# Two-layer text-and-image attention: five value products instead of six for two entries, image tokens first in every other entry, small work moved between VectorE and GpSimd, and a new order of the first groups

## The chip, the cores and the metric

The kernel runs on one core of one Trainium2 chip, in one launch. The metric is the device time of the execution in microseconds; the figure of a kernel is the median of its runs. The engines are TensorE (PE; PEld is its weight load), VectorE (DVE), ScalarE (ACT), GpSimd (POOL) and SyncE (SP, which only issues DMAs here).

## The reference

Two layers of cross attention run one after the other on `x`, 16 entries of 256 tokens by 320 channels, with 20 heads of 16. Each entry has a context of 256 tokens by 512; in layer 0 its first 77 tokens are text and the other 179 are image tokens, in layer 1 the last 4 are image tokens. This is layer 0, shortened:

```python
text, ip = ctx[:, :77], ctx[:, 77:]
q = x @ Wq; k_text = text @ Wk; v_text = text @ Wv
text_out = softmax(q_h @ k_h.T * scale) @ v_h                 # by head
ip_k = ip @ Wk_ip; ip_v = ip @ Wv_ip
text_probs = softmax(q @ k_text.T * scale)                    # all channels
sem = (text_probs @ text) @ ip.T * scale                      # query x image token
ip_out = (softmax(q_h @ ip_k_h.T * scale + 0.5 * sem) * mask) @ ip_v_h
out = (text_out + ip_out) @ Wout + bout + x
```

Layer 1 has the same form with a normalized `sem`.

## The kernel before, in words

Numbers are fp32, and most products are made of fp32r halves: a value is rounded to a high part by ACT and the rest is its low part, a subtraction on DVE or POOL (`halves` L162, `split` L280). `prod` (L236) then makes high x high, high x low and low x high; over 512 channels, four blocks of 128, that is 12 matmuls.

**Layer 0 by groups.** A group k is four heads of one entry (5 groups an entry, 80 in layer 0). `slot0` (L785) writes the PE order out by hand: the scores of group k+2 (`score0` L739), whose maxima DVE takes from PSUM for text and image tokens apart; the turned scores of group k (`turned0` L760: token by query), to which the maxima have been added as rows by a DMA (`maxima0` L750); exp on ACT; a factor on POOL (L776) that carries `sem`; and the values of group k-1 (`attend0` L778, three blocks V of tokens times P), which DVE transposes and divides by the sums in `settle0` (L813) before POOL adds text and image into `hsn`. The values have one PSUM bank, P, for all groups, so the next group's values wait until the last reader of the bank is done. The scores have one bank pair, S.

**What is prepared meanwhile.** Two entries (a pair c) share the products of the context. The tasks of a pair are spread over the groups ahead by due times (`task`, L1149 on; `shifted(n, ...)` is in groups relative to the pair's first one, n = 10 c), and `fill` runs what is due: `k0` loads the context (`context` L265, tiles `cta` and `ctb`, split whole in 512 columns: text and image of one entry, then of the other) and makes the keys (`keys0` L367), which go out to DRAM (`kd`) and back as rows of `ks`; `q0` the queries (`queries0` L647, `hq` being x in halves), out to `qd` and back into `qs`; `v0` the values of one entry (`values0_` L419): three products of 128 context rows by 320 columns, rows 0 to 127 with the text weights, the same rows with the image weights, and rows 128 to 255 with the image weights; in the first two a mask per row (`tmask`) drops the tokens of the other kind; `m0t` the token product M (`tokens0` L431); `s0` the factor (`semantic0` L654). `c0` (`finish` L839) splits the finished heads of an entry into `ho` and makes the output product (`project` L604, L611).

**Order.** PE's order is the program's. In `begin` (L1247), which is all that comes before group 0's slot, the order of SP, ACT, DVE and POOL is the program's too; after it a scheduler sets the order of these, but instructions marked `queued` stay behind the last `anchor` of their engine (a maximum on DVE, an exp on ACT, a factor on POOL). SP issues in order, and a DMA whose data isn't ready holds up those behind it. In `begin`, `stacks0` loads the rows of a group in parts: K (keys), Q (queries), T and M (the factor's rows).

**Layer 1** has no products of that kind; its value step (`settle1` L998) ends with a copy of the last block of `hsn` on POOL.

## Time and profile before

| | |
|---|---|
| median of 3 runs (lowest to highest) | 1493.27 us (1488.1 to 1494.71) |
| profiled execution, its span | 1491.16 us, 1489.3 us |
| granted clock of PE over the span | 0.984 |
| instructions | 36118 |
| first turned scores of group 0 | 56.62 us |
| ten groups of layer 0 (group 34 to 44, first turned matmul each) | 74.50 us |
| HBM read, written | 118.04 MB, 77.04 MB |

The span is that of the profiled execution and begins with its first instruction. Times in rows of the profile are microseconds from there. A row of a timeline or of the chain gives start and length, then engine, line and tiles (written <- read) and how many; a row of a group gives busy us and the mean ns of one instruction, and behind the second bar the idle time of the engine ahead of it with what ended it. A matmul's length in a group runs from its issue to its end, and several are under way at once, so what it costs the path is read from the chain.

### The profile page before, as it was taken

The page shows a single profiled execution, that of the slowest core. Times are in us where ns is not written, and L with a number is a line of the kernel's source. Part 1 is how long each engine was busy: PE and PEld are TensorE (multiplying, and loading weights), DVE is VectorE, ACT ScalarE, POOL GpSimd, SP SyncE. Part 2 cuts the span into 40 slices and gives each one's busy share as a digit, 9 for nine tenths or more (in the row PEclk, how much of TensorE's full clock was granted, in tenths as well). Part 3 has the DMA queues.
Part 4 walks back from the last instruction along what each step waited for, and adds up shares of the span by engine and source line. Part 5 has one row for each costly group of instructions (what it writes and reads, how often), then busy time and mean ns, then how long its engine had stood idle before and what let it go on. Part 6 is the DMA issues. An engine that isn't in the chain of part 4 may idle for free.

```text
span 1489.3 us, 36118 instructions
## 1 busy us (share of the span) xinstructions
PE 1426.1 (96%) x12740; PEld 1155.8 (78%) x12740; DVE 1172.7 (79%) x2595; ACT 886.0 (59%) x1975; POOL 1212.5 (81%) x1302
## 2 busy tenths in 40 slices
PE   8799999999999899789999999999999999999998
PEld 7678888888888788577777777777777777777766
DVE  5467777777777787778887788788878887888787
ACT  5346565656565555456665666566666665666563
POOL 4359797979797877798698779878987898788887
PEclk9799999999999999799999999999999999999999
DMA  7867777778787776684534444444444444444411
GB/s 237 212 178 222 205 223 205 222 204 224 200 228 202 208 204 176 165 222 151 155 104 126 123 117 119 133 122 116 121 133 119 121 121 124 125 122 102 112 32 55
DMA packets 230986, 234.32 MB, mean 157 GB/s; under 512 B 39127, under 2 KB 200678, under 8 KB 230790
## 3 DMA queue, kind: packets, MB, share of 16 engines
q1 hardware_dynamic: 228598, 230.71, 55.8%
q8 instruction: 102, 1.67, 0.5%
q10 hardware_dynamic: 2208, 1.30, 0.4%
q14 instruction: 78, 0.64, 0.1%
HBM read 118.04 MB, written 77.04 MB: 131 GB/s over the span
## 4 chain that ended last, share of the span: by engine, by line
PE 75%; DVE 8%; DMA 5%; POOL 5%; issue 3%; ACT 3%; SPq 1%; ACTq 0%; DVEq 0%; POOLq 0%
PE X L944 15%; PE X L241 14%; PE P L805 6%; PE X L611 5%; PE S L746 5%; PE P L956 5%; PE P L966 4%; PE T L770 4%; PE T L895 3%; PE S L901 3%; PE X L614 2%; PE X L251 2%; PE X L580 2%; DVE mn L748 2%; POOL P L776 1%
## 5 line engine op out<-in xcount | busy, mean ns | idle before, releaser
L776 POOL TENSOR_TENSOR P<-P,rs 128x512 f32<-128x512 f32 x320 | 414.4, 1318 | 86.6 <-ACT P L773 79.8
L935 POOL TENSOR_TENSOR wt<-P,ctb 128x512 f32<-128x512 f32 x318 | 408.4, 1308 | 74.1 <-ACT ctb L933 74.0
L944 PE MATMUL X<-ctb,gm 128*128 128x512 f32 x1120 | 306.3, 402 | 5.8 <-DVE wt L945 5.7
L773 ACT ACTIVATE P<-T 128x512 f32<-128x512 f32 x320 | 175.4, 594 | 159.4 <-PE T L770 112.4
L945 DVE TENSOR_TENSOR wt<-X,wt 128x512 f32<-128x512 f32 x320 | 216.1, 681 | 42.2 <-PE X L944 37.3
L944 PEld LDWEIGHTS X<-ctb,gm 128*128 128x128 f32 x1120 | 195.0, 188 | 39.3 <-DVE wt L945 8.7
L915 ACT ACTIVATE P<-T 128x512 f32<-128x512 f32 x320 | 173.1, 593 | 75.1 <-PE T L895 72.1
L933 ACT ACTIVATE ctb<-P 128x512 fp32r<-128x512 f32 x320 | 186.6, 627 | 38.0 <-PE X L944 35.2
L903 DVE TENSOR_REDUCE mn<-S 128x4 fp32r<-128x1008 f32 x160 | 191.5, 1197 | 0.0
L748 DVE TENSOR_REDUCE mn<-S 128x4 fp32r<-128x716 f32 x160 | 142.4, 890 | 0.0
L805 PE MATMUL P<-P,vr 128*32 128x256 f32 x1920 | 125.9, 393 | 6.1 <-DVE tmp L822 2.2
L746 PE MATMUL S<-ks,qs 125*128 125x256 f32 x640 | 117.4, 307 | 6.2 <-DMA ks<-M 4.1
L746 PEld LDWEIGHTS S<-ks,qs 125*128 125x128 f32 x640 | 89.0, 195 | 40.8 <-issue 22.1
L1035 POOL TENSOR_TENSOR r<-u,rs 128x40 f32<-128x40 f32 (+2 forms) x17 | 108.7, 6395 | 3.1 <-DVE u L1032 3.0
L770 PE MATMUL T<-qs,ks 127*128 127x256 f32 x640 | 107.7, 291 | 0.4 <-DMA qs<-mt 0.3
L747 DVE TENSOR_REDUCE mn<-S 128x4 fp32r<-128x308 f32 x160 | 74.5, 466 | 31.1 <-PE S L746 31.0
L816 DVE STREAM_TRANSPOSE nt<-P 128x512 f32<-128x512 f32 x80 | 57.1, 713 | 52.9 <-PE P L805 52.2
L805 PEld LDWEIGHTS P<-P,vr 128*32 128x32 f32 x1920 | 56.7, 112 | 47.4 <-POOL P L776 7.3
L770 PEld LDWEIGHTS T<-qs,ks 127*128 127x128 f32 x640 | 91.6, 197 | 1.7 <-DMA qs<-mt 0.8
L956 PE MATMUL P<-P,v1t 128*32 128x256 f32 x1280 | 85.7, 385 | 0.0
L966 PE MATMUL P<-wt,zone 128*32 128x256 f32 x1280 | 84.4, 379 | 0.0
L241 PE MATMUL X<-wC,cta 128*128 128x324 f32 (+1 forms) x474 | 78.4, 312 | 0.0
(305 smaller groups left out, 2976.8 us busy)
## 6 DMA issues: line engine op xcount, KB each, us to landing
qd<-q SPq DMA_DIRECT2D x96, 256.0 KB
qs<-tph SPq DMA_DIRECT2D x64, 320.0 KB
rawc<-in_cT_dram SPq DMA_DIRECT2D x60, 256.0 KB
qs<-qd SPq DMA_DIRECT2D x80, 192.0 KB
ks<-kd SPq DMA_DIRECT2D x80, 192.0 KB
ks<-kd SPq DMA_DIRECT2D x160, 96.0 KB
qs<-qd SPq DMA_DIRECT2D x160, 96.0 KB
kd<-kst SPq DMA_DIRECT2D x57, 256.0 KB
```

What stands on the lines that cost most here:

```text
L241: last = mm(out, lhs(a, k), rhs(b, k), start=i == 0, stop=i == len(terms) - 1)
L746: mm(sp[:, h], Q[: XROW + T0, h, t * 128 : (t + 1) * 128], K[: XROW + T0, h], start=True, stop=True)
L770: mm(st[p][:, j], K[:KS0, 2 * p + j, t * 128 : (t + 1) * 128], Q[:KS0, 2 * p + j], start=True, stop=True)
L773: exp = anchor(nc.scalar.activation(pt, st[p], AF.Exp, scale=SCALE))
L776: anchor(nc.gpsimd.tensor_mul(pt, pt, rs[:, t : t + 1].to_broadcast([128, 2, S])))
L805: mm(pv[32 * s : 32 * s + 32, o : o + S], v[:, vt, h : h + 32], P[k, s // 2][:, t, s % 2], start=vt < 2, stop=vt != 1,)
L903: anchor(nc.vector.tensor_reduce(maxes[k + 2][:, t], sp[:, :, :T1], axis=AX.X, op=ALU.max))
L915: anchor(nc.scalar.activation(P[k, u][:, t], st[u], AF.Exp, scale=SCALE))
L933: nc.scalar.activation(R[k, u][:, t], P[k, u][:, t], AF.Copy, scale=0.5)
L935: anchor(eng.tensor_sub(W[k, u][:, t], P[k, u][:, t], f(R[k, u][:, t])))
L944: mm(yp, gm[:, gb], R[k, u][:, kt], start=i == 0, stop=i == len(blocks[n]) - 1)
L945: nc.vector.tensor_mul(W[k, u][:, n], yp, W[k, u][:, n])
```

## The change

**Context layout.** `cta` and `ctb` hold, for high and low part each, the text columns of both entries (2 x 77) and the image columns of both (2 x 179) with 26 zeroed columns between the two image parts. The split therefore runs in two pieces, text and image (each with one ACT and one POOL or DVE instruction; `begin` likewise). The text keys take 154 columns, the token product 180 instead of 192.

**Values.** In even entries the image tokens come first: tokens 0 to 127 of the image, then 51 image and 77 text tokens. In odd entries it is 77 text and 51 image tokens, then 128 image tokens. The 51 image rows of both lie in one tile of 128 rows, so one product (`vm`) makes both; each entry keeps a text product and one of 128 image rows. The masks of V are written per entry by POOL (`mark`, two copies), where `marks` wrote them once.

**Order of tokens.** For even entries the key stacks are read at an offset of 77 columns (`turned_ks`), the maxima change sides, and the values take the blocks image, mixed image, text. M's zero columns are set once and no longer by a memset for each entry.

**Keys.** The image parts of `kst` are evacuated in two pieces, the copy of the text keys to `kb` is made by two instructions.

**Between engines.** In `settle0` the product goes to the values' bank and a DVE sum over it writes `hsn` (twice in the last group of an entry, for POOL's copy). The last block of `hq` is subtracted by POOL on 64 partitions, where DVE made one instruction on 128. In layer 0 the low part of `ho` is made by POOL (`split_pool`). In layer 1 the last group writes both copies in one DVE product.

**The start.** The second entry's products stand between the scores of groups 0 and 1; the writes of its queries (`held`) and of its keys come behind the maxima of group 1; the second pair's splits move out of `begin` into group 0.

```diff
     def evacuate(hi, lo, out, m, pieces=None):
+        cut = [lambda t, b=b: t[:, b] for b in pieces] if pieces else [lambda t: t]
...
+        for of in cut:
+            nc.scalar.copy(of(hi), of(out[:64] if m == 2 else out))
...
+        for of in cut:
+            nc.vector.tensor_sub(of(out if m == 2 else lo), of(out), f(of(hi)))
```
```diff
+    def value_rows(ct, at, w, *to):
+        vp = bank()[:, :320]
+        prod(vp, lambda s, k: side(ct[k], s, at, 128), lambda s, k: w(s, k), 4)
+        for V, t, sc in to:
             nc.scalar.activation(
                 vcols(V, V0W)[:, t, :, 0:16], vp.rearrange("p (h d) -> p h d", d=D), AF.Copy, scale=sc
             )
     def values0_(b):
         ct, i = ct0[b // 2], b % 2
-        V = vr[(b + 2) % 3]
-        for t, (w,), lo, sc in ((0, wv0, 0, tmask[:, 0:1]), (1, wvi0, 0, tmask[:, 1:2]), (2, wvi0, 128, 1.0)):
...
+        V = mark(b)
+        value_rows(ct, T0 if i else -MIX, wv0[0], (V, 0, masks(b)[0]))
+        yield
+        value_rows(ct, CI + (CG + MIX if i else 0), wvi0[0], (V, 2, 1.0))
+        yield
         return V
+    def values_mixed(c):
+        to = [(vr[(b + 2) % 3], 1, masks(b)[1]) for b in (2 * c, 2 * c + 1)]
+        value_rows(ct0[c], CI + 128, wvi0[0], *to)
+        yield
```
```diff
-        tmp = buf("tmp", [128, 2, 8, 16], bufs=2)
-        nc.vector.tensor_mul(tmp, nt[:, :, :, 0:16], rz.unsqueeze(3).to_broadcast([128, 2, 8, 16]))
-        nc.gpsimd.tensor_add(hn[:, g // 2, :, g % 2], tmp[:, 0], tmp[:, 1])
+        tmp = pv[:, 16:272]
+        nc.vector.tensor_mul(
+            tmp.rearrange("p (a f d) -> p a f d", a=2, f=8), nt[:, :, :, 0:16], rz.unsqueeze(3).to_broadcast([128, 2, 8, 16])
+        )
+        tmp = tmp.rearrange("p (a f d) -> p f d a", a=2, f=8)
         if g == NG - 1:
-            nc.gpsimd.tensor_copy(hn[:, 2, :, 1], hn[:, 2, :, 0])
+            for i in range(2):
+                nc.vector.tensor_reduce(hn[:, 2, :, i], tmp, axis=AX.X, op=ALU.add)
             later(0.45, lambda: gather(0, b))
+        else:
+            nc.vector.tensor_reduce(hn[:, g // 2, :, g % 2], tmp, axis=AX.X, op=ALU.add)
+    def split_pool(src, neg, tag):
+        hl = buf(tag, [128, 5, S], FR)
+        nc.scalar.copy(hl[:, 0:2], src[:, 0:2])
+        nc.scalar.activation(hl[:, 2], src[:, 2], AF.Copy, scale=neg)
+        nc.gpsimd.tensor_sub(hl[:, 3:5], src[:, 0:2], f(hl[:, 0:2]))
+        nc.gpsimd.tensor_add(hl[:, 2], src[:, 2], f(hl[:, 2]))
+        return hl
```
```diff
-        task(("v0", 2 * c), shifted(n, -7, -5.4, -5), lambda b=2 * c: values0_(b), *k)
-        task(("v0", 2 * c + 1), shifted(n, -4, -3.8, -3.4), lambda b=2 * c + 1: values0_(b), *k)
+        task(("v0", 2 * c), shifted(n, -7, -5.4), lambda b=2 * c: values0_(b), *k)
+        task(("vm", c), shifted(n, -4.2), lambda c=c: values_mixed(c), *k)
+        task(("v0", 2 * c + 1), shifted(n, -3.8, -3.4), lambda b=2 * c + 1: values0_(b), ("vm", c))
```
```diff
         stacks0(1, "TQK")
-        parts(v0)
         get(*v0)
+        parts(vm)
+        stacks0(2, "KQ")
+        parts(q1)
+        score0(0, 0)
+        stacks0(2, "TM")
         parts(v1)
-        stacks0(2, "KQ")
-        score0(0, 0)
-        parts(q1)
-        stacks0(2, "TM")
+        score0(0, 1)
         get(*q1)
         parts(s1, s1, s1)
-        score0(0, 1)
+        stacks0(3, "KQ")
+        maxima0(0, nc.sync)
+        stacks0(3, "TM")
         parts(k1)
         parts(s1, s1)
-        parts(k0)
-        parts(v1)
-        maxima0(0, nc.sync)
-        parts(s1)
+        score0(1, 0)
         parts(v1)
         get(*v1)
-        score0(1, 0)
-        parts(k1)
         parts(s1)
-        stacks0(3)
-        parts(k1)
         score0(1, 1)
-        parts(k1, k1)
+        parts(s1)
         maxima0(1, nc.sync)
+        for make in held:
+            make()
+        parts(k0)
         resid0.append(load(xT_d[0], "xc"))
```

More of the change, by code (lines that the diff above doesn't have):

```diff
@@ L200, in in_turn @@
             if i:
-                halves(*ahead.pop(0), eng, wait)
+                hi, lo, src = ahead.pop(0)
+                if isinstance(hi, list):
+                    for piece in zip(hi, lo, by_side(src)):
+                        halves(*piece, eng, "pieces")
+                else:
+                    halves(hi, lo, src, eng, wait)
             for j in new:
@@ L301, in xattn2 @@
     for k in range(4):
-        first["c", k] = cT_d[k * 128 : (k + 1) * 128, : 2 * S], ct[k][:, 0], ct[k][:, 1], ("rawc", "raw")[k // 2]
+        first["c", k] = cT_d[k * 128 : (k + 1) * 128, : 2 * S], *[[of(ct[k], s) for of in (texts_of, images_of)] for s in range(2)], ("rawc", "raw")[k // 2]
         first["k", k] = rows(wk0_d, k), *rounded(wkt[:, k]), "P"
@@ L396, in keys_first @@
         out = lambda lo, hi: bank()[:, : 2 * (hi - lo)].rearrange("p (b t) -> p b t", b=2)
-        kp = [out(0, T0 + 1) for m in range(3)]
+        kp = [out(0, T0) for m in range(3)]
         for k in range(4):
@@ L616, in project, with queries @@
             yield
-    def queries(l, a):
+    def queries(l, a, held=None):
         qh = buf("q", [128, 2, 3, S], FR)
+        send = lambda out, in_: dma(out, in_) if held is None else held.append(lambda: dma(out, in_))
         def evac(m, pp):
@@ L649, in queries0 @@
         yield
-        xs = split(x, tmask[:, 5:6], nc.gpsimd, "hq") if b else xs0.pop()
+        xs = split(x, None, nc.gpsimd, "hq") if b else xs0.pop()
         yield
-        return (yield from queries(0, xs))
+        return (yield from queries(0, xs, held if b == 1 else None))
     def semantic0(b):
@@ L1264, in high @@
             for n in names:
-                nc.scalar.copy(first[n][1], view(n))
+                for hi, src in zip(first[n][1], by_side(landed[n])) if n[0] == "c" else ((first[n][1], view(n)),):
+                    nc.scalar.copy(hi, src)
         def low(*names, eng=nc.vector):
             for n in names:
+                if n[0] == "c":
+                    for hi, lo, src in zip(first[n][1], first[n][2], by_side(landed[n])):
+                        eng.tensor_sub(lo, src, f(hi))
+                    continue
                 lo = first[n][2]
```

207 lines of the change are left out of this document (132 added, 75 removed).

## The prediction

> **What bounds the kernel now.** I read the busy shares first, then the same engines by stage (windows), then the chain of waits inside one stage, and last the groups of that stage.
>
> ```profile
> PE 1426.1 (96%) x12740; PEld 1155.8 (78%) x12740; DVE 1172.7 (79%) x2595; ACT 886.0 (59%) x1975; POOL 1212.5 (81%) x1302
> ```
> ```profile
> 0.00:60.00 60.00, 46.51 (x273) 43.46 (x274) 32.06 (x94) 30.86 (x80) 19.74 (x43) 0.92 0.84 239
> ```
> ```profile
> 337.23:367.60 30.37, 30.14 (x287) 25.95 (x286) 23.50 (x57) 19.70 (x48) 30.32 (x29) 1.00 0.81 233
> ...
> 322.67:397.17 74.50, 73.44 (x702) 63.60 (x701) 57.95 (x137) 44.31 (x105) 65.72 (x65) 1.00 0.78 214
> 500.00:690.00 190.00, 168.03 (x1506) 137.50 (x1508) 149.19 (x330) 100.92 (x238) 154.65 (x175) 0.93 0.69 190
> 690.00:1489.00 799.00, 783.70 (x6953) 605.47 (x6943) 661.08 (x1403) 499.96 (x1062) 661.92 (x725) 1.00 0.41 116
> ```
> ```profile
> by line: PE X L241 23.6%; PE P L805 17.4%; PE S L746 15.6%; PE T L770 11.3%; PE X L611 8.1%; issue 3.2%; PE X L668 3.1%; PE X L251 2.9%; PE X L614 2.4%; DVE mn L748 2.2%; PE X L754 1.5%; ACT cta L166 1.4%; ACT ho L284 1.0%; DVE ho L285 0.9%
> ```
>
> The windows give, after the length, busy us of PE, PEld, DVE, ACT and POOL, then clock and DMA share. There are four regimes. Up to 60 us the start: PE is idle for 13.5 us. Then layer 0, which repeats every two entries; one period is 74.50 us (322.67 to 397.17), with PE busy 73.44. From 500 to 690 us the weights of layer 1 come in on top, and PE has 22 us of idle time. From 690 us layer 1, PE busy 784 of 799. The by-line row is the chain of the one period: nearly all of it is PE, with X L241, the products of the context, as its largest line. So in layer 0 time taken from PE is time taken from the span, as long as nothing else is as full. One thing is: in the stretch 337.23 to 367.60 (groups 36 to 39 of that period), POOL is busy 30.32 of 30.37 us, beside a full PE. That is where this change is decided.
>
> **The change part by part.**
>
> *One value product fewer for two entries (PE, removed).* Each entry had three products of 12 matmuls over 320 columns; the mixed rows of two entries now share one, so two entries need five instead of six.
>
> ```profile
> 326.47 3.52 PE X L241 x24
> ...
> 387.88 2.86 PE X L241 x24
> ```
> ```profile
> L241 PE MATMUL X<-wD,cta 128*128 128x320 f32 x24 | 4.2, 309 | 0.0
> ```
>
> The first row, from the chain, is two such products in a row: 3.52 / 24 = 0.147 us a matmul on the path (the 309 ns of the group row is its length from issue to end, and neighbours overlap). A product is 12 x 0.147 = 1.76 us. The second row is one product of 320 columns behind one of the token product's 192 columns, so the latter has (2.86 - 1.76) / 12 = 0.091 us each; at 180 columns I estimate 0.086, 0.12 us for two entries. Seven of the eight pairs lie in layer 0's periods (the first is in the start, below): 7 x 1.88 = 13.2 us of PE work less. The Trainium skill, "TensorE: Matmul & The Clock Gate", section Back-to-back issue gap, gives N / 2.4 + 2.5 ns for a lone warm matmul, so 136 ns at 320 columns; the row's 147 ns is longer, and by the page the seven products would be worth 11.4 us instead of 12.3.
>
> *GpSimd (POOL): low parts in, sums out.* Groups of the one period:
>
> ```profile
> L776 POOL TENSOR_TENSOR P<-P,rs 128x512 f32<-128x512 f32 x42 | 54.2, 1315 | 7.8 <-ACT P L773 7.7
> L823 POOL TENSOR_TENSOR hsn<-tmp 128x128 f32<-128x128 f32 x10 | 5.1, 508 | 0.5 <-DVE tmp L822 0.5
> ...
> L285 POOL TENSOR_TENSOR hq<-xq,hq 128x512 fp32r<-128x512 f32 x2 | 2.6, 1290 | 0.0
> L386 POOL CAST kb<-kst 128x308 fp32r<-128x308 f32 x2 | 0.9, 440 | 0.0
> L825 POOL COPY hsn<-hsn 128x128 f32<-128x128 f32 x2 | 0.6, 289 | 0.0
> L436 POOL MEMSET M<- 77x154 f32 x2 | 0.5, 227 | 0.5 <-PE X L698 0.5
> ```
>
> Removed per period: 10 sums of 0.508, 2 copies of 0.289, 2 memsets of 0.227: 6.1 us. Added: two low parts of ho, each 512 elements (1.29, as hq) and 256 elements, which lie between the 128-element and the 512-element row; on their line (2.04 ns an element) 0.77. Together 2 x 2.06 = 4.1. The last block of hq twice: I take 0.77 for it too, bounds 0.51 and 1.29, 1.5. Context splits in two pieces (154 and 358 elements, 0.56 + 0.98 on the line) in place of one of 512: 0.25 x 4 = 1.0. The key casts in halves, 128 elements being 0.289 and 308 being 0.440: 0.18 x 3 = 0.5. Four marks of 20 columns, about a memset each: 0.9. Added 8.0, net +1.9 us per period on 65.7.
>
> *VectorE (DVE).* Groups of the same period:
>
> ```profile
> L747 DVE TENSOR_REDUCE mn<-S 128x4 fp32r<-128x308 f32 x20 | 9.3, 466 | 2.0 <-PE S L746 1.8
> ...
> L285 DVE TENSOR_TENSOR ho<-hT,ho 128x512 fp32r<-128x512 f32 x2 | 2.3, 1165 | 1.4 <-ACT ho L284 1.4
> L286 DVE SCALAR_TENSOR_TENSOR ho<-ho,tmask,hT 128x256 fp32r<-128x256 f32 x2 | 2.2, 1102 | 0.0
> L286 DVE SCALAR_TENSOR_TENSOR hq<-hq,tmask,xq 128x256 fp32r<-128x256 f32 x2 | 1.3, 640 | 0.0
> ```
>
> It loses 5.8 us of ho and hq and gets 12 sums over 256 elements out of PSUM. No row shows that sum; it lies between nothing and the 0.466 of 308 elements, I take 0.41 (nearest is the product of the same size below, 0.41): 4.9 us. With image parts evacuated in two pieces (about +0.4) it comes out even, at 58 of 74.5 busy; hidden behind PE. The values' bank is held 0.4 us longer per group. Tightest is the group whose values start at 369.54:
>
> ```profile
> 368.28 0.41 DVE L822 TENSOR_TENSOR tmp<-nt,P 128x256 f32<-128x256 f32 x1
> ```
>
> The bank is free 0.85 us ahead there, and a sum of 0.41 fits unless DVE puts a maximum (0.9) between: 0 to 0.5 us a period, I take 0.
>
> ACT gets some ten short instructions more, 1.3 us by its like ones, at 44 of 74.5 busy: hidden, but for one place (0.4, next part).
>
> *Where POOL has no room.* POOL last waits ahead of the full stretch at the first row, then runs without a gap to the end of the third; the last row (chain) is the value product that reads what that writes.
>
> ```profile
> 335.30 2.81 POOL L776 TENSOR_TENSOR P<-P,rs 128x512 f32<-128x512 f32 x2 [0.69 <-ACT P L773]
> ...
> 346.51 0.92 POOL L823 TENSOR_TENSOR hsn<-tmp 128x128 f32<-128x128 f32 x1
> ...
> 363.91 5.08 POOL L776 TENSOR_TENSOR P<-P,rs 128x512 f32<-128x512 f32 x4
> ```
> ```profile
> 369.54 1.43 PE P L805 x24
> ```
>
> The last factor is done at 368.99; the last 8 of the 24 matmuls, which need it, start two thirds in, at 370.5: room 1.5 us. New work in that queue: both hq blocks 1.5, one ho 2.06, four context splits 1.0, one cast 0.2, two marks 0.45: 5.2. Gone: four sums (one of them took 0.92), one copy, one memset: 2.8, and some 0.6 by which products were stretched beside DVE's hq and ho (the 2.81 beside 2.54, half of 5.08, and two more like it). Net 1.8 against a room of 1.5: PE waits 0.3 us per period here. Also PE takes the second half of P 8 matmuls (0.48 us) earlier in even entries; the tightest groups there wait on ACT, not POOL, and I count 0.
>
> ```profile
> 384.01 1.20 PE L611 MATMUL X<-ho,wF 128*128 128x256 f32 x8 [0.81 <-ACT mt L756]
> ```
>
> Here PE waits on ACT, which evacuates keys just before; two pieces more there and ho in two instructions cost about 0.4. Per period then -1.88 + 0.3 + 0.4 = -1.2, times 7 = -8.3 us. In 500 to 690 PE is not alone on the path, and about half of the last pairs' share is lost there: +1, so -7.3.
>
> *The start.* Issues on SP, and what PE waits for:
>
> ```profile
> 40.18 3.99 SPq L86 DMA_DIRECT2D qd<-q  x5
> ...
> 46.20 1.96 SPq L86 DMA_DIRECT2D rawc<-in_cT_dram  x2
> 48.20 0.91 SPq L86 DMA_DIRECT2D raw<-in_cT_dram  x2
> 49.16 2.61 SPq L86 DMA_DIRECT2D kd<-kst  x4
> 52.34 1.28 SPq L86 DMA_DIRECT2D kd<-ho  x2
> 53.73 2.58 SPq L758 DMA_DIRECT2D qs<-mt  x4
> ```
> ```profile
> 48.76 0.41 PE L754 MATMUL X<-ident_r,mn 128*8 128x128 f32 x2
> ...
> 56.62 1.35 PE L770 MATMUL T<-qs,ks 127*128 127x256 f32 x4
> ```
> ```profile
> 53.43 1.28 DVE L169 TENSOR_TENSOR cta<-rawc,cta 128x512 fp32r<-128x512 f32 x2
> ```
>
> Group 0 turns at 56.62, after its maxima have landed. They were ready for SP soon after 48.76, but were issued at 53.73, behind the second pair's loads and the second entry's keys; the second entry's five query writes stood further ahead. All of these (10.8 us of issues) now come behind them; ks<-kd and qs<-qd of group 3 (two issues) come ahead. What is late next is PE's own order: the scores of group 1 and its maxima come before the turn, with one product fewer ahead. I put the turn 5 us earlier, bounds 0 and 7. Given back: the second pair's splits (2.6 us on DVE, two pairs like the row) move into group 0, among its maxima, and the held writes and the keys' writes, 7.9 us of issues, stand ahead of the stacks of group 4: 1 us, bounds 0 and 5. Net -4.
>
> *Layer 1* loses 16 copies on POOL and gets 16 wider products on DVE, both off PE's path: 0.
>
> **Sum:** -7.3 - 4 = -11.3 on the profiled execution, 1491.2 us with what lies around its span of 1489.3. That gives 1479.9 for an execution like the profiled one, and 1482 beside the median of 1493.3. I forecast 1480.
>
> **The rivals.**
>
> *POOL does not bind* (against it: 30.32 of 30.37). For it:
>
> ```profile
> L945 DVE TENSOR_TENSOR wt<-X,wt 128x512 f32<-128x512 f32 x320 | 216.1, 681 | 42.2 <-PE X L944 37.3
> ```
>
> 512 elements with one source in PSUM take DVE 0.681, those of ho with both in SBUF 1.165, and the sum of 0.92 on POOL (0.508 in the mean) runs beside them: the two engines hold each other up, and with ho off DVE both win. Then 7 x 1.88 = 13.2, and 0.7 a period (the 0.9% of the chain on DVE ho) x 7 = 4.9, less 0.4 x 7 on ACT, and 6 for the start: 1491.2 - 21.3 = 1470. The Trainium skill, "SBUF — State Buffer", section Who interferes with whom, says that a DVE instruction with two SBUF inputs locks out a GpSimd instruction that reads SBUF, and the loser blocks; by that rule this case is what comes out, and the one row of 0.92 us agrees with it.
>
> *POOL takes it all back* (for it: with the three 256-element blocks of the full stretch at their upper bound the net there is 1.8 + 1.6 = 3.4 against a room of 1.5; against it: the same relief of POOL). PE waits 1.5 us or more a period instead of 0.3. The periods give nothing, the start 4: 1487.
>
> *Slower: ho's low part comes too late.* On DVE it ended 2.5 us before PE took it in one entry, and just before in the other:
>
> ```profile
> 347.02 0.68 DVE L286 SCALAR_TENSOR_TENSOR ho<-ho,tmask,hT 128x256 fp32r<-128x256 f32 x1
> ...
> 381.96 1.52 DVE L286 SCALAR_TENSOR_TENSOR ho<-ho,tmask,hT 128x256 fp32r<-128x256 f32 x1
> ```
> ```profile
> 350.19 0.95 PE X L611 x8
> ```
>
> POOL runs in order. If it takes ho behind the four factors of a group (5.1 us) instead of ahead, PE, also in order, stops at L611 in both entries: about 2.5 us each. With one entry hit that is 7 x (2.5 - 1.2) - 4 = +5, 1496; with both 7 x (5 - 1.2) - 4 = +23, 1514. The change is slower from 1.8 us a period on. Against it: the scheduler puts an instruction where it is ready, and ho is ready ahead of the factors.
>
> **How the numbers follow.** Forecast (1480) 0.45, POOL not binding (1470) 0.25, all back (1487) 0.17, ho late (1496 to 1514) 0.13. The range 1466 to 1494 takes in the first three with the start's bounds and the unknown rows. Half a per cent, about what a measurement of this kernel can tell from no change, is 7.5 us, so faster means under 1485.8: nearly all of the first two, 0.67; the same 0.20; slower 0.13.
>
> **What would show it.** The period (T to T, ten groups) falls from 74.5 to about 73.2; six products of 320 columns become five; POOL over 66 of it; the turn of group 0 at 51 to 53; idle time of PE in front of L611 on ho from POOL would be the slower rival, in front of the values from POOL the second. I am wrong if the period stays while PE is busier than its matmuls need, or if the start's turn does not move.

## The result

The changed kernel is slower: 1502.56 us (1499.71 to 1509.03) against 1492.39 us (1486.92 to 1497.81) for the kernel before, seven runs each, ratio 1.0075 with a 95% interval of 1.0051 to 1.01. The forecast was 1480, the range ended at 1494. The profiled execution took 1503.56 us, its span is 1501.8.

First the busy row of its page, then the same engines by stage (length, busy us of PE, PEld, DVE, ACT and POOL, clock, DMA share), at the places that were shown for the kernel before. The second stage is again groups 34 to 44, the third again groups 36 to 39.

```profile
PE 1413.3 (94%) x12644; PEld 1141.8 (76%) x12644; DVE 1181.3 (79%) x2676; ACT 892.8 (59%) x2047; POOL 1209.6 (81%) x1324
```
```profile
0.00:60.00 60.00, 43.86 (x268) 41.10 (x268) 30.41 (x98) 31.59 (x90) 23.88 (x74) 0.94 0.78 214
330.15:406.61 76.46, 72.25 (x691) 62.08 (x690) 58.71 (x143) 45.42 (x114) 65.14 (x66) 1.00 0.78 207
344.04:376.93 32.89, 30.55 (x286) 26.10 (x285) 22.90 (x58) 19.71 (x53) 30.29 (x31) 1.00 0.80 218
500.00:690.00 190.00, 165.83 (x1510) 135.68 (x1503) 148.80 (x344) 101.55 (x246) 153.09 (x165) 0.95 0.75 192
```

PE did become lighter: 72.25 us of a period instead of 73.44. But the period grew from 74.50 to 76.46, so PE stands still for 76.46 - 72.25 = 4.21 us of it where it stood for 1.06. POOL is no longer full in its tight stretch (30.29 of 32.89, before 30.32 of 30.37). So the question is who now holds PE up. PE's waits in this period (line waited on, releaser: us in total, times, longest):

```profile
PE X L707 <- ACT mt L852: 1.3, 1, 1.3
PE X L252 <- DVE sp L765: 1.1, 1, 1.1
PE P L901 <- DVE mx L768: 0.7, 1, 0.7
PE X L704 <- ACT mt L852: 0.5, 1, 0.5
PE P L901 <- DVE hsn L927: 0.5, 1, 0.5
```

The kernel before has one wait in its period, 0.8 us on ACT's maxima at L611 (now L704). Three new ones stand beside it: the values (P, L901) wait for VectorE, the token product (L252) for the semantic scores `sp`, and the second half of the output product (L707) for the maxima that ACT evacuates (`mt`).

Where the 12.5 us of span came from, by the first turned matmul of groups 4 and 78 (96.7 and 675.9 us before, 98.1 and 685.8 after):

| stretch | before | after | forecast of the difference | measured |
|---|---|---|---|---|
| start to group 4 | 96.7 | 98.1 | -4 | +1.4 |
| group 4 to group 78 | 579.2 | 587.7 | -7.3 | +8.5 |
| group 78 to the end | 813.4 | 816.0 | 0 | +2.6 |

The runs of one kernel lie some 10 us apart, so the last row says little; the middle one is the case.

### The profile page after: what moved, and what is told of

Same layout as the page of the kernel before. It is cut to its first block, busy times and chain, and to the rows that moved or that the text cites. A ratio compares the mean times of both kernels' runs of the same rounds, so it can differ in the third digit from the quotient of the medians.

```text
span 1501.8 us, 36240 instructions
## 1 busy us (share of the span) xinstructions
PE 1413.3 (94%) x12644; PEld 1141.8 (76%) x12644; DVE 1181.3 (79%) x2676; ACT 892.8 (59%) x2047; POOL 1209.6 (81%) x1324
## 3 DMA queue, kind: packets, MB, share of 16 engines
q1 hardware_dynamic: 228614, 230.71, 56.7%
## 4 chain that ended last, share of the span: by engine, by line
PE 68%; DMA 9%; DVE 8%; POOL 7%; ACT 3%; issue 3%; SPq 1%; ACTq 1%; POOLq 0%; DVEq 0%
PE X L1054 15%; PE X L252 12%; PE P L901 5%; PE P L1066 5%; PE X L704 5%; PE P L1076 4%; PE T L1005 3%; PE S L841 3%; PE S L1011 3%; POOL P L872 3%; PE T L866 2%; DMA qs<-qd 2%; PE X L262 2%; PE X L707 2%; DVE mn L844 2%
## 5 line engine op out<-in xcount | busy, mean ns | idle before, releaser
L872 POOL TENSOR_TENSOR P<-P,rs 128x512 f32<-128x512 f32 x320 | 407.6, 1295 | 110.6 <-ACT P L869 108.8
L901 PE MATMUL P<-P,vr 128*32 128x256 f32 x1920 | 126.9, 394 | 16.4 <-DVE hsn L927 8.1
L901 PEld LDWEIGHTS P<-P,vr 128*32 128x32 f32 x1920 | 57.6, 112 | 58.1 <-POOL P L872 16.0
L272 ACT CAST kst<-X 128x179 fp32r<-128x179 f32 (+5 forms) x117 | 36.2, 329 | 86.2 <-PE X L252 47.1
```

Of the source, the lines that this page charges most:

```text
L872: anchor(nc.gpsimd.tensor_mul(pt, pt, rs[:, t : t + 1].to_broadcast([128, 2, S])))
L901: mm(pv[32 * s : 32 * s + 32, o : o + S], v[:, vt, h : h + 32], P[k, s // 2][:, t, s % 2], start=bool(start), stop=bool(stop),)
```

## The experiments

Two theories stood at the beginning. **Theory V:** VectorE's sum holds the values' bank P longer, and PE waits for it. **Theory G:** the low parts that GpSimd took over delay the splits of the context, with them the loads, ACT's casts and the maxima. Each kernel below was timed beside the kernel before on the same chip, whose medians were 1494.26 (first four), 1493.04 (next four), 1494.35 (next four), 1492.57 (next four) and 1494.67 us (last two). Differences below are between these medians, and carry the 2 us by which those of the kernel before differ. "Ten groups" is a quarter of the time between the first turned matmuls of groups 14 and 54 in the trace; it is 74.6 us in the kernel before and 77.0 in the changed one.

| kernel | median us | ratio to before, interval | ten groups |
|---|---|---|---|
| changed kernel | 1502.56 | 1.0075 (1.0051 to 1.01) | 77.0 |
| sums_back | 1531.92 | 1.0249 (1.0217 to 1.0282) | 81.0 |
| ho_back | 1495.46 | 1.0011 (0.9991 to 1.003) | 75.2 |
| small_back | 1510.42 | 1.0094 (1.006 to 1.0128) | 76.8 |
| start_back | 1509.92 | 1.0097 (1.0064 to 1.0131) | 77.2 |
| sum_sbuf | 1487.03 | 0.9956 (0.9936 to 0.9976) | 74.4 |
| ho_sbuf | 1486.77 | 0.9962 (0.9943 to 0.998) | 73.5 |
| sixth | 1499.49 | 1.0032 (1.0016 to 1.0049) | 76.0 |
| ho_hq_back | 1499.90 | 1.0053 (1.0032 to 1.0074) | 75.6 |
| sixth_sbuf | 1485.92 | 0.9941 (0.992 to 0.9962) | 74.5 |
| before_hold | 1517.53 | 1.0158 (1.0123 to 1.0193) | 78.7 |
| before_sbuf | 1510.34 | 1.0105 (1.0069 to 1.0141) | 77.5 |
| noanchor_sbuf | 1487.93 | 0.9956 (0.9929 to 0.9983) | 74.6 |
| sp_act | 1495.47 | 1.0015 (0.9992 to 1.0038) | 75.0 |
| sp_sixth | 1496.16 | 1.002 (1.0 to 1.0041) | 75.5 |
| ho_sp | 1499.95 | 1.005 (1.0028 to 1.0073) | 75.5 |
| start_sbuf | 1491.88 | 0.9989 (0.9966 to 1.0012) | 74.8 |
| sp_reduce | 1481.56 | 0.9914 (0.988 to 0.9948) | 73.4 |
| reduce_sixth | 1488.04 | 0.9958 (0.9936 to 0.9979) | 74.4 |

### One part undone at a time

**sums_back**: the sums on GpSimd again.

```diff
-        tmp = pv[:, 16:272]
+        tmp = buf("tmp", [128, 2, 8, 16], bufs=2)
...
+        nc.gpsimd.tensor_add(hn[:, g // 2, :, g % 2], tmp[:, 0], tmp[:, 1])
...
-            nc.vector.tensor_reduce(hn[:, g // 2, :, g % 2], tmp, axis=AX.X, op=ALU.add)
```

> The changed kernel with one part undone: text and image are added by GpSimd from an SBUF tile again, not by a VectorE sum over the values' bank. Theory V (the VectorE sum holds the values' bank and delays the banks behind it: PE waits some 2.8 us more a period on DVE's instructions): those waits go, a period falls from about 76.4 to 74 us and the time from 1502.6 to about 1487. Theory G (GpSimd's work for ho and hq is what delays the context and the maxima): GpSimd gets 5.7 us a period on top, and the time stays or rises, 1503 to 1512.

**ho_back**: ho's low part on VectorE again.

```diff
-        hh = split(hT, tmask[:, 6:7], nc.vector, "ho") if l else split_pool(hT, tmask[:, 6:7], "ho")
+        hh = split(hT, tmask[:, 6:7], nc.vector, "ho")
```

> The changed kernel with one part undone: in layer 0 the low part of ho is made by VectorE again. Theory V: VectorE has 4.5 us a period more beside the sums, its waits grow: 1503 to 1512. Theory G: GpSimd has 4.1 us a period less, the context splits and with them the loads and ACT's casts come earlier: 1490 or less.

**small_back**: the two edits above, and hq's last block back on VectorE; only the new layout and the new start stay.

```diff
-        xs = split(x, None, nc.gpsimd, "hq") if b else xs0.pop()
+        xs = split(x, tmask[:, 5:6], nc.gpsimd, "hq") if b else xs0.pop()
```

> The changed kernel with all three moves between engines in layer 0 undone (sums, ho, hq). The context's layout, the product fewer and the new start stay. If the moves cause the loss, in whichever way: period 73 to 74 us and a time of about 1482 to 1486. If the layout itself (splits in two pieces, ordered as anchors) or the new start causes it: the time stays above 1495.

**start_back**: the old order of the first groups.

```diff
-        return (yield from queries(0, xs, held if b == 1 else None))
+        return (yield from queries(0, xs, None))
...
         parts(vm)
+        parts(v1)
         stacks0(2, "KQ")
+        score0(0, 0)
         parts(q1)
-        score0(0, 0)
...
-        for make in held:
-            make()
-        parts(k0)
```

> The changed kernel with the order of the start as it was (second entry's keys and queries sent where they were, second pair's splits in the start). The profile shows group 0's turn only 1.5 us earlier and groups 1 and 2 longer by 6.5 us. If that order costs: 1497 or less. If it is neutral: 1502 with a turn at about 56.6.

PE's longest waits from 160 to 480 us in sums_back:

```profile
PE X L704 <- POOL ho L930: 11.8, 4, 3.0
PE X L707 <- DVE xc L956: 7.2, 4, 2.4
```

And in small_back:

```profile
PE X L704 <- ACT ho L326: 5.0, 4, 1.3
```

sums_back shows the wait of the forecast's slower rival: with sums and low parts both in its queue, GpSimd delivers ho up to 3.0 us late, about once a period. More comes beside it (7.2 us on `xc`), and its 1532 lies above that rival's 1514, above theory G's 1503 to 1512 and far from theory V's 1487. Undoing ho brings 7 us; that is theory G's direction, but not its 1490 or less. But small_back, which undoes all that was moved, is slower than ho_back by 15 us: PE waits for the high part of ho, which ACT makes from the finished heads, and these come from the sums in GpSimd's queue. (Its profiled execution took 1499.73 us, its median is 1510.42, so these rows show only part of the loss.) The kernel before has the same chain without such a wait; what in the new layout or the new start brings it out is not shown. So the new layout with the work on its old engines loses. start_back is taken up in "The start".

### The bank, and the product

**sum_sbuf** changes one line of the changed kernel: the product goes to SBUF, and VectorE sums from there, so P is free one instruction earlier. **ho_sbuf** adds the edit of ho_back.

```diff
-        tmp = pv[:, 16:272]
+        tmp = buf("tmp", [128, 2, 8, 16], bufs=2).rearrange("p a f d -> p (a f d)")
```

> The changed kernel with one thing undone: the products with the reciprocals go to a buffer in SBUF again, and VectorE adds the two halves from there, so the values' bank comes free after the products and not after the sums. Theory V (the bank held by VectorE's sum costs PE): the waits of the values (P) for hsn of L927, 1.8 us in 320 us, and about half of those for mx of L768, 3.2 us, go; with four periods in that stretch some 0.8 us a period, times 7, so 1497 where the changed kernel has 1502.6; at most 5.0 / 4 x 7 = 9 us. Theory G (GpSimd's added work delays the context's splits) alone: no change, within 3 us of 1502.6, the waits for sp of L765 and for mt of L852 stay. If VectorE's sum with both inputs in SBUF is held up beside GpSimd, as the old low part of ho was (1165 ns for 512 elements), VectorE's sum takes longer than 0.41 us and the gain goes in part.

> Both undone: ho's low part on VectorE (as in ho_back, 1495.5 us) and the products in SBUF with the sum on VectorE. Theory G gives 7 us of this again, theory V about 5.5 us of bank waits in four periods, 1.4 x 7 = 10 us at most, so 1486 to 1492; periods of 73.5 to 74.5 where ho_back has 74.4 to 77. If the bank has no price: 1495. The rival that VectorE becomes too full (it has the sums and ho's low part): 1497 or more, with PE waiting for VectorE's ho at L704.

**sixth** puts a sixth product back into the changed kernel. Nobody reads its result, so it is work added.

```diff
+        if not i and b:
+            value_rows(ct, CI + 128, wvi0[0])
+            yield
...
-        task(("v0", 2 * c), shifted(n, -7, -5.4), lambda b=2 * c: values0_(b), *k)
+        task(("v0", 2 * c), shifted(n, -7, -5.4, -5), lambda b=2 * c: values0_(b), *k)
```

> The changed kernel with the removed product put back without use: a sixth value product of 12 matmuls over 320 columns for each later pair of entries, whose result nobody reads. It sizes what the product is worth on PE. If PE is the bound in the changed kernel as in the one before, 7 x 12 x 0.147 = 12.3 us: 1515. If the new waits of PE (4.6 us a period) are what sets the pace, the product falls into them in part: 1503 to 1509.

**ho_hq_back** has the edits of ho_back and of hq.

> ho's low part and the last block of hq's low part on VectorE again, the sums on VectorE as in the changed kernel. GpSimd then has 6 us a period less than the changed kernel. Theory G with hq counted: below ho_back's 1495.5 by 2 to 4 us, as two blocks of 0.73 us leave the full stretch of GpSimd. The rival, that GpSimd is no longer the bound once ho is off it and VectorE is next: 1495 to 1502, with PE waits for VectorE's q of L329 or ho of L704.

One line brought 15.5 us, more than the whole loss and more than the 9 us at most that was expected. This is the place in the changed kernel's timeline (start and length, engine, line; only the rows that matter):

```profile
406.36 0.42 DVE L918 TENSOR_TENSOR P<-nt,P 128x256 f32<-128x256 f32 x1
...
406.89 0.47 DVE L843 TENSOR_REDUCE mn<-S 128x4 fp32r<-128x308 f32 x1
...
407.28 0.89 DVE L844 TENSOR_REDUCE mn<-S 128x4 fp32r<-128x716 f32 x1
...
408.09 0.41 DVE L927 TENSOR_REDUCE hsn<-P 128x128 f32<-128x256 f32 x1
...
408.65 1.07 PE L901 MATMUL P<-P,vr 128*32 128x256 f32 x16 [0.82 <-DVE mx L768]
```

The sum itself takes 0.41 us, as worked out. But VectorE does not run it behind the product: the maxima of a later group come between, and the bank, whose last reader had been the product at 406.78, is free at 408.50. PE has nothing else in its order and stands. (The profile puts the end of the wait down to the maximum L768 that happened to end last; the reader of the bank is L927.) PE's waits for the values in layer 0, 96 to 690 us, in the kernel before:

```profile
PE P L805 <- DVE tmp L822: 2.2, 2, 1.8
PE P L805 <- DVE mx L675: 2.2, 1, 2.2
PE P L805 <- POOL P L776: 1.5, 2, 0.9
```

In the changed kernel:

```profile
PE P L901 <- DVE hsn L927: 7.0, 9, 2.6
PE P L901 <- DVE mx L768: 4.0, 5, 0.8
PE P L901 <- DVE mx L769: 2.3, 1, 2.3
PE P L901 <- POOL P L872: 1.6, 4, 0.6
```

In sum_sbuf:

```profile
PE P L901 <- DVE tmp L918: 2.9, 2, 2.1
PE P L901 <- POOL P L872: 1.7, 3, 0.6
```

5.9, 14.9 and 4.6 us: the bank's own waits explain 10 of the 15.5 us. Another 3.9 us are waits of the scores for rows of queries (`qs<-qd`, six in the changed kernel), of which sum_sbuf has none. No single wait shows the rest. (The two profiled executions are 17.7 us apart between groups 4 and 78, a little more than the medians.)

Theory V carries most. Theory G's share hangs on the bank: with the bank held, taking ho off GpSimd brings 7 us, with the bank free nothing in the total (1487.03 and 1486.77). ho_sbuf has the shorter period (73.5 against 74.4), but loses it between groups 64 and 78, 126.5 us against 116.8: there its granted clock is 0.89 against 0.93, and the same 906 matmuls keep PE busy for 107.1 us against 100.5. Why the clock is lower was not followed up. ho_hq_back (1499.9, bank held) is slower than ho_back (1495.5), so hq's block does less harm on GpSimd than on VectorE, against what theory G expected of it.

The sixth product cost nothing: 1499.5 against 1502.6. That speaks against the largest term of the forecast, 12.3 us of matmuls.

### The same parts on the kernel before

**before_hold** and **before_sbuf** change nothing but the sums in the kernel before: to VectorE, out of the bank (the product written to `pv[:, 16:272]`) or out of SBUF. **sixth_sbuf** is sum_sbuf with the edit of sixth. **noanchor_sbuf** is sum_sbuf with the pieces of the splits placed more freely.

```diff
-        nc.gpsimd.tensor_add(hn[:, g // 2, :, g % 2], tmp[:, 0], tmp[:, 1])
+        tmp = tmp.rearrange("p a f d -> p f d a")
...
+            nc.vector.tensor_reduce(hn[:, g // 2, :, g % 2], tmp, axis=AX.X, op=ALU.add)
```
```diff
-            order = lambda inst: anchor(queued(inst))
+            order = queued
```

> The kernel before with one part of the change alone: VectorE sums the halves out of the values' bank, in place of GpSimd out of SBUF; layout, start and low parts as before. Theory V: the bank is held 0.8 us longer per group (a product and a sum, a maximum between them at worst), which in the changed kernel cost 15.5 us: 1499 to 1508 less what GpSimd's relief gives back, so above 1497. The rival, that the price of the bank hangs on the new layout or on GpSimd's low parts: 1485 to 1493.

> The kernel before with the sums on VectorE, but out of SBUF: GpSimd loses 5.7 us a period, VectorE gains 4.9, the bank is not held longer. PE is idle for 1.06 us of a period of 74.50 there, and GpSimd was full in one stretch, so at most 7 us of gain: 1486 to 1492 if GpSimd's full stretch held PE up, 1493 if PE alone is the bound. Above 1496 only if VectorE becomes too full. If it is as fast as sum_sbuf (1487.0), the new layout itself gives nothing.

> sum_sbuf (1487.0 us) with the unused sixth product of each later pair of entries put back. With the bank held it cost nothing (1499.5 against 1502.6). Theory V: once the bank is free PE is the bound again, and the product costs its 7 x 12 x 0.147 = 12.3 us: 1499. The rival: the product has no price even there, because PE still waits 2.5 us in a period of 74.4 (309.3 busy in 320 us) and takes it in these gaps: 1487 to 1491.

> sum_sbuf with the pieces of the context's splits on GpSimd given their places as freely as one whole split was, so that they are no longer fixed points for what comes after. The waits left in sum_sbuf are for sp of L765 (4.5 us in four periods) and for mt of L852 at L707 (3.5 us); if they come from where the splits stand in GpSimd's queue, 2 us a period go at most: 1475 to 1483. If they come from ACT's own order (the casts of the context stand ahead of mt whenever the load lands there), no change: 1485 to 1490.

Holding the bank costs 7 us on the old layout too (1517.5 against 1510.3), and both kernels are slower than expected. But the sums on VectorE are no gain there even out of SBUF: my 1486 to 1492 was wrong by 18 us. PE's longest waits in before_sbuf from 160 to 480 us say why:

```profile
PE X L251 <- DVE q L169: 6.5, 5, 1.3
PE X L241 <- DVE sp L671: 3.4, 4, 1.0
```

VectorE has the sums on top of ho and hq now and is late with what PE reads next: from group 34 to 44 it is busy for 66.26 of 77.34 us, in the kernel before for 57.95 of 74.50. More than the sums is in this: the 512-element row of ho takes it 2336 ns in the mean (160 to 480 us), 1164 in the kernel before. In the new layout VectorE can carry sums and ho together (ho_sbuf, 1486.8, busy for 62.24 of 73.05). What makes room there, hq's block on GpSimd, the new layout or the product less, no run separates. noanchor_sbuf changed nothing (1487.9); that was expected if the wait for `mt` comes from ACT's own order.

sixth_sbuf again: 1485.9 with the product, 1487.0 without. PE's work in the period shows that it is there. The periods of sum_sbuf and of sixth_sbuf (groups 34 to 44):

```profile
319.07:393.75 74.68, 71.70 (x691) 61.74 (x689) 58.67 (x146) 44.79 (x114) 65.78 (x67) 1.00 0.80 214
```
```profile
317.75:392.71 74.96, 73.14 (x702) 63.41 (x701) 58.85 (x146) 45.49 (x114) 65.69 (x67) 1.00 0.81 212
```

With the product PE is idle for 1.82 us, without it for 2.98. So most of what was taken out turned into waiting, and sum_sbuf's timeline has two places with a wait of over 1 us. The first, ahead of the token product, whose bank VectorE must have emptied of `sp`:

```profile
356.95 0.89 DVE L844 TENSOR_REDUCE mn<-S 128x4 fp32r<-128x716 f32 x1
...
357.76 0.23 DVE L765 TENSOR_TENSOR sp<-sp,X 128x77 f32<-128x77 f32 x1
...
358.05 0.43 PE L252 MATMUL X<-cta,wB 128*128 128x360 f32 x1 [1.06 <-DVE sp L765]
```

VectorE takes a group's maxima first (0.46 and 0.89), and 0.23 us of `sp` behind them. In sixth_sbuf PE does not wait here, but not because the sixth product fills the place. The product stands some four groups earlier: there PE has 24 matmuls in a row, sum_sbuf has 12, and the second twelve are the first two rows below. At the token product VectorE takes `sp` ahead of the same maxima:

```profile
323.14 1.04 PE L252 MATMUL X<-wD,cta 128*128 128x320 f32 x6
324.01 1.04 PE L252 MATMUL X<-wD,ctb 128*128 128x320 f32 x6
...
356.29 0.24 DVE L768 TENSOR_TENSOR sp<-sp,X 128x77 f32<-128x77 f32 x1 [0.54 <-ACT sp L767]
...
357.14 0.47 DVE L846 TENSOR_REDUCE mn<-S 128x4 fp32r<-128x308 f32 x1
```

So the added product changed the order on VectorE as well, and the pair compares two orders, not one product alone. The second place is on ACT:

```profile
348.67 0.71 ACT L172 CAST ctb<-rawc 128x154 fp32r<-128x154 f32 x2 [1.53 <-DMA rawc<-in_cT_dram]
349.40 0.36 ACT L852 CAST mt<-X 8x256 fp32r<-8x256 f32 x1
```

A cast that waits 1.53 us for a load stands ahead of the maxima `mt`, which PE awaits at L707. SP issues this load at 344.96, behind GpSimd's splits of the tile before (341.21 to 343.89) and, in its own order, behind two writes of queries (342.85 to 344.87). In ho_sbuf the splits begin at 339.83, the loads are issued at 341.23 and 343.13, and the wait at L707 is not there; PE waits for `mt` only 0.5 us at L704 and 0.3 at L792 in that period. That is theory G's chain, but only this much of it, and that the load waits for the buffer which the splits free is inferred from these times.

### The wait for sp

Further kernels took the wait at L252 away, each on top of sum_sbuf: the bank is emptied by ScalarE. **sp_act** and **ho_sp** (on ho_sbuf) copy twice and add two SBUF operands; **sp_sixth** is sp_act with the sixth product.

```diff
-            nc.vector.tensor_add(sp, sp, sf[:, :T0])
+            st = buf("st", [128, T0], bufs=2)
+            nc.scalar.copy(st, sf[:, :T0])
+            nc.vector.tensor_add(sp, sp, st)
```

> sum_sbuf, and the semantic scores leave their bank by two copies of ScalarE (0.22 us each), VectorE adds them out of SBUF. If the wait at L252 is what takes up the product's place, 1.1 us a period times 7, some 8 us, go: 1479. If the next wait comes in its stead (ScalarE's mt at L707, VectorE's q at L762) or ScalarE's two more copies an entry delay the maxima: 1485 to 1489.

> sp_act with the unused sixth product put back. If the product has its price once nothing else stands in its place: sp_act + 12, some 1491. If the period is set by a chain beside PE: within 3 us of sp_act.

> ho_sbuf (1486.8) with the semantic scores emptied by ScalarE as in sp_act. ho_sbuf has no wait at L252 left, so no gain from it there: 1485 to 1489. Faster than sp_act by some 5 us only if the wait for mt at L707 (3.5 us in four periods in sum_sbuf, 1.7 in ho_sbuf) is what is left over.

All three are 8 to 13 us slower than the same kernel without this edit; sp_act and ho_sp missed what was expected. sp_sixth came out as its second case, within 3 us of sp_act, so the product cost nothing here either. The row of `sp` on VectorE (160 to 480 us) in sum_sbuf and in sp_act:

```profile
L765 DVE TENSOR_TENSOR sp<-sp,X 128x77 f32<-128x77 f32 x18 | 4.2, 233 | 2.0 <-ACT sp L764 1.6
```
```profile
L767 DVE TENSOR_TENSOR sp<-sp,st 128x77 f32<-128x77 f32 x18 | 20.0, 1109 | 2.3 <-ACT st L766 2.3
```

The same 77 elements take 1109 ns where both operands lie in SBUF, 233 ns where one lies in PSUM. **sp_reduce** therefore makes one copy of both halves and adds by a reduction, which has one operand; **reduce_sixth** puts the sixth product on top.

```diff
-            nc.scalar.copy(sp, sf[:, NT : NT + T0])
-            nc.vector.tensor_add(sp, sp, sf[:, :T0])
+            st = buf("st", [128, 2, T0], bufs=2)
+            nc.scalar.copy(st, sf[:, : 2 * NT].rearrange("p (s n) -> p s n", s=2)[:, :, :T0])
+            nc.vector.tensor_reduce(sp, st.rearrange("p s n -> p n s"), axis=AX.X, op=ALU.add)
```

> sum_sbuf (1487.0); the semantic scores leave their bank by one copy of ScalarE of both halves, and VectorE adds them out of SBUF by a reduction with one operand (like the sums: 0.42 us for 256 elements from SBUF, 0.42 from the bank), some 0.3 us in place of the 1.11 of sp_act. If the wait for sp at L252 (1.1 us a period) is what is late: 1479 to 1483. If another wait takes its place, 1485 to 1490. If ScalarE's emptying is itself what VectorE's sums need to wait for, or the reduction takes over 1 us: as sp_act, 1495.

> sp_reduce with the unused sixth product. The product has its price of 12.3 us where PE is the bound: sp_reduce + 8 to 12. If it costs under 4 us here too, the period of 74 us is set by a chain beside PE, and PE's busy share of 96% does not make it the bound.

The rows of the reduction and of the sums out of SBUF, and the period, in sp_reduce, then the period of reduce_sixth:

```profile
L766 DVE TENSOR_REDUCE sp<-st 128x77 f32<-128x154 f32 x18 | 5.7, 316 | 1.3 <-ACT st L765 0.6
...
L928 DVE TENSOR_REDUCE hsn<-tmp 128x128 f32<-128x256 f32 x35 | 14.8, 423 | 0.6
```
```profile
319.27:392.55 73.28, 71.48 (x691) 61.67 (x689) 58.95 (x146) 45.18 (x114) 65.73 (x67) 1.00 0.81 218
```
```profile
318.65:392.66 74.01, 73.19 (x703) 63.45 (x701) 59.23 (x146) 45.52 (x114) 65.58 (x67) 1.00 0.81 215
```

316 ns instead of 1109, the wait at L252 is gone, and sp_reduce is the fastest kernel of the study: 1481.56 us, 0.9914 (0.988 to 0.9948) of the kernel before, as expected if that wait is what is late; its interval overlaps sum_sbuf's a little. It has the change whole, with the two banks emptied early. And here the product has a price at last: 6.5 us between the medians, less than the 8 to 12 expected for a PE that is the bound and more than the 4 of a chain beside PE (the intervals overlap a little). It is 1.0 us for ten groups in the mean and 0.73 in the period shown, where PE is busy for 1.71 more. PE's waits in this period say where the rest is, in sp_reduce

```profile
PE X L707 <- ACT mt L853: 1.3, 1, 1.3
PE X L704 <- ACT mt L853: 0.5, 1, 0.5
```

and in reduce_sixth, whose lines stand three further down:

```profile
PE X L707 <- ACT mt L856: 0.5, 1, 0.5
PE X L710 <- ACT mt L856: 0.3, 1, 0.3
```

The wait of 1.3 us at the second half of the output product shrinks to 0.3: ACT begins the cast of `mt` at 349.52 in one and at 349.48 in the other, and PE, behind the product, comes to it later. So one more us of the product lies in a wait.

One execution was profiled of each kernel, and from group 4 to group 78 the four pairs differ by -1.4 us (sixth), 5.7 (sixth_sbuf), -0.6 (sp_sixth) and 13.1 (reduce_sixth). The medians differ by -3.1, -1.1, 0.7 and 6.5. Only in the last pair do both say that the product costs, and there this stretch of layer 0 shows the whole price.

### The start

**start_sbuf** is sum_sbuf with the edit of start_back.

> sum_sbuf with the start's old order. Forecast of the start's gain: 4 us; with the bank held the old order cost 7.3 (1509.9 against 1502.6). So 1491 to 1495, with the turn of group 0 at 58 to 60 us in place of 53.9. If the turn alone moves and the load of the next groups takes it back: 1487 to 1489.

The new order is worth 4.9 us here and 7.4 on the changed kernel (1509.9 against 1502.6; 3.3 if the ratios are compared), near the 4 of the forecast. For start_back neither case that was expected (1497 or less, 1502) came true: the old order loses. Yet the changed kernel, which turns group 0 at 55.1 us, reaches group 4 later than the kernel before. SP's issues ahead of the turn:

```profile
49.88 2.61 SPq L854 DMA_DIRECT2D qs<-mt  x4
...
54.52 1.27 SPq L90 DMA_DIRECT2D rawc<-in_cT_dram  x2
```

The loads of the second pair do stand behind the maxima now, which SP issues at 49.88 instead of 53.73. But with the old order the rest of the change turns group 0 at 59.4 us where the kernel before turned at 56.6, and reaches group 4 at 100.9 against 96.7; by that the gain of the order is gone. Of these 4 us, 2.8 are there at the turn, ahead of any sum. Ahead of the turn start_back has PE wait 7.3 us for its first weights (5.9 in the kernel before), and GpSimd busy for 8.80 of the first 10 us (6.07 before). What follows the turn can come from the sums: before_hold and before_sbuf, with the old layout, turn at 56.7 and 56.8 and reach group 4 at 99.0 and 99.5. The granted clock from 50 to 60 us differs too (0.83 in the kernel before, 1.00 in the changed one, 0.67 in start_back); its share is not separated.

## Why the prediction was wrong

- **The values' bank: the step that failed.** The prediction had the wait, its place and its bounds ("unless DVE puts a maximum (0.9) between: 0 to 0.5 us a period, I take 0"). The runs say 1.2 us a period in the waits shown (0.7 + 0.5), 10 us of waits in layer 0 against sum_sbuf, and 15.5 us in all. Two things were off: a maximum does come between, and more than one instruction of 0.9 us fits in, because the sum is free to slip behind whatever VectorE has ready; and I looked at the tightest group of the kernel before instead of at any group whose next values stand right behind.
- **What is left beside the bank.** With the bank free (sum_sbuf) the kernel takes 1487.0 us, where 1482 was forecast beside the median. The next points name what this rest can consist of; no run splits it.
- **The product: its size on PE was right, its worth on the path was not.** PE fell from 73.44 to 71.70 us a period in sum_sbuf, 1.74 for the 1.88 of the forecast. But a period with PE busy for 73.44 of 74.50 us does not mean that what is taken from PE is taken from the period. The prediction asked what is late next for the start and not for the periods: in sum_sbuf PE then waits 1.06 us for `sp` and 1.4 for `mt`. Worth by the medians: nothing in three kernels, some 6.5 us in the fourth. How much of the nothing is waiting and how much a changed order on VectorE stays open.
- **GpSimd: the added work was put too high, and it is not the bound.** The rows of the period:

```profile
L872 POOL TENSOR_TENSOR P<-P,rs 128x512 f32<-128x512 f32 x40 | 50.6, 1285 | 9.7 <-ACT P L869 9.4
L934 POOL TENSOR_TENSOR ho<-hT,ho 128x512 fp32r<-128x512 f32 x2 | 2.6, 1290 | 0.0
...
L935 POOL TENSOR_TENSOR ho<-hT,ho 128x256 fp32r<-128x256 f32 x2 | 1.5, 738 | 0.1
L329 POOL TENSOR_TENSOR hq<-xq,hq 64x256 fp32r<-64x256 f32 x2 | 1.5, 730 | 0.2
```

  The estimates of 0.77 for the 256-element blocks came out as 0.738 and 0.730. The split in two pieces (887 and 512 ns) costs little more than the one of 1377 or 1292, where 0.25 us each was forecast. The factors take 51.61 of GpSimd's 65.72 us in the period before and 50.01 of 65.14 in this one; the work beside them thus went from 14.1 to 15.1, by 1.0 where 1.9 was forecast, and the shorter factors take that back. In the tight stretch the parts named as gone add up to 3.0 us (3 x 0.508 + 0.92 + 0.289 + 0.227), not 2.8, so the wait there comes to 0.1 us by the prediction's own rows. PE has no wait on POOL in the period: the 0.3 us, and the rival in which POOL takes all back, did not happen.
- **ACT's place** (L611, now L704) was put at 0.4 us more a period; there the wait for `mt` fell from 0.8 to 0.5. Instead PE waits 1.3 us for `mt` at another place, the second half of the output product, where a cast that waits 1.39 us for its load stands ahead of `mt` in the changed kernel too. The sum had no term for this.
- **The start:** the order's gain and what is given back were about right (5 at the turn, measured 4.3 and 5.6). What the rest of the change costs in the start, 2.8 us at the turn, was not in the sum.
- **The slower rival** covers the measured time with its 1496 to 1514, but that is luck: PE never waits for ho from GpSimd in the changed kernel. Its wait appeared in sums_back, where the sums stay in GpSimd's queue.
- **The rival that POOL does not bind** saw the relief rightly: from 160 to 480 us the factors take 1313 ns in the kernel before and 1286 in the changed one, and 1304 and 1317 where ho is on VectorE again (ho_back, ho_sbuf). But the relief is 2%, and PE's new waits were for VectorE and ACT, so its 1470 did not follow.

## What to carry to other kernels

An operation that moves to another engine also moves the moment at which its input's buffer comes free; ask not how long it takes but what the scheduler may put in front of it, and release a bank that PE waits for with the shortest possible last reader. Work taken from the busiest engine is worth only what the waits behind it leave of it: look for the waits behind it first, since a kernel at 96% gave nothing for 12 us of matmuls in three runs of four. An edit that adds or takes out work can change the order on other engines too, so look at both timelines before the difference is called the price of that work. When a change of several parts loses, vary one line at a time: here the sums tried alone on the kernel before lost, and the whole change with one line changed won.

## What the runs showed of the hardware

Two additions on VectorE of the same 77 elements differ by the place of one operand: 233 ns in the mean with one in PSUM, 1109 ns with both in SBUF, beside a GpSimd that is busy for 277 of 320 us. The single instances of the latter spread widely; sp_act's row of them (160 to 480 us; least, median and greatest ns):

```profile
L767 DVE TENSOR_TENSOR sp<-sp,st x18: 667/714/2841, 174.8 to 476.0; 128x77 f32<-128x77 f32 x18
```

A reduction with its one operand in SBUF isn't slowed: the 423 ns of the sums in sp_reduce stand beside 419 ns out of the bank in the changed kernel:

```profile
L927 DVE TENSOR_REDUCE hsn<-P 128x128 f32<-128x256 f32 x34 | 14.2, 419 | 0.8
```

The Trainium skill, "SBUF — State Buffer", section Who interferes with whom, says that a VectorE instruction with two SBUF inputs contends with a GpSimd instruction that reads SBUF, and that one with at most one SBUF input, outside certain faster modes, does not. These rows agree with it.

How long a VectorE instruction with two SBUF operands takes differs from kernel to kernel: the 512-element row of ho took 1164 ns in the kernel before, 931 in ho_sbuf and 2336 in before_sbuf (means, 160 to 480 us). Why is not shown.
